# Softplus terms summed by TensorE in the first batch, and two scan carries copied at once, in a two-layer vision network on one core

## The chip, the cores and the metric

The kernel runs on one core of one Trainium2 chip. The metric is the device time of one execution in microseconds, as the median of repeated runs. All matrices are FP32.

## What is computed

The network has two layers; each mixes positions and then channels, with residuals between. Only the first half of layer 0 is touched here. It is a selective scan in four directions (k = 0 to 3) over an image of 32 x 32 positions (L = 1024), with D = 384 channels and N = 16 states, for a batch of 4:

```python
x_dbl = einsum('bkdl,kcd->bkcl', xs, x_proj_weight)      # 12 + 16 + 16 rows
dts   = einsum('bkrl,kdr->bkdl', x_dbl[:, :, :12], dt_projs_weight)
dt    = softplus(dts + dt_projs_bias)
# scan over l, for every channel d and state n:
h = h * exp(dt * A) + (dt * u) * B ;  y = sum_n h * C
```

After the scan come a merge of the four directions, a LayerNorm and a GELU. The rest of the network is a mixture of experts (two of four experts per token), an attention with eight heads, and a factored feed-forward. This document calls that rest of a batch its tail.

## The kernel before

**Units.** The scan layer works through 32 units in order: batch b (4), direction k (4), half of the positions i (2, each HF = 512 wide). The two halves of one direction follow each other. The first starts from a zero state and stores the last state of every block in `carry`; the second starts from `carry`. So units 0, 2, 4 and so on (the first-half units) copy carries, and units 1, 3, 5 do not. Units 0 to 7 are the first batch.

**Inside a unit** (`chunk`). Three chunks of 128 channels; in each, four groups g of four states. In a group, a tile covers 32 channels x 4 states on 128 partitions, and there are four blocks of 512 positions, in two pairs q:

- GpSimd (POOL) makes `bx = dtr * B` for both blocks of a pair in one instruction (L408). `bx` has six buffers, so three groups can be under way.
- ScalarE (ACT) makes `da = exp(dtr * nega)` for one block, into PSUM (L417; two banks).
- VectorE (DVE) runs the scan of one block (L422). For q = 0 the state goes over `bx`, for q = 1 over `da`.
- For q = 0, in a first-half unit, VectorE copies the last column of each of the two blocks from `bx` to `carry` (L433, one element per partition, SBUF to SBUF, one instruction a block); then POOL multiplies both blocks by C in place (L436). For q = 1 VectorE copies the last column from `da` in PSUM (L428) and multiplies by C itself (L429).
- TensorE (PE) sums the states with a selection matrix into the accumulator `acc` (L443), which frees `bx`. At the end of a chunk VectorE adds `acc` into `y` (L282, L286).

**One unit ahead** (`project`). While a unit is scanned, a generator prepares the next one. It is advanced once per group. Its first step makes the 44 rows of `x_dbl` (L318, copied by L322) and sends B and C through DRAM (`bcs`). Then, for each of three chunks of channels, it makes dt and dt * u. `begin` issues a product into the PSUM tile `ps` (L344) and six activations (L347 to L352). With z the biased product, m = exp(-|z|) and e = 1 + m, softplus is relu(z) + ln(e) + (m - (e - 1)); the last bracket gives back what was rounded off e. One group later POOL does the two subtractions (L364, L365). One group after that VectorE adds the result to relu (L370) and multiplies by u (L371), ACT copies dt out (L372), and the SP queue stores both to DRAM (L373, L374), from where the next unit's `dtr` tiles are loaded (L392). So the project part of units 1 to 7 is issued inside units 0 to 6, and that of unit 0 before the loop, with no scan beside it. Unit 7 prepares the first unit of the second batch.

**What sets the order.** The instructions of each engine are put in order when the kernel is built, by a scheduler that goes by the program's order as priority and by times that it estimates; on the chip each engine works through its list in that order. `behind` (`issue_after`) puts the POOL subtractions and the VectorE pair of `project` behind the latest group's own instruction on that engine. The product L344 and the activations have no such rule. After a batch's scan its tail is issued too, in part with raised priority, and runs beside the scan of the batches after it. The tail of the last batch has nothing beside it.

**Room.** The tag `ps` has two PSUM banks, for `acc`, `dt_ps`, `xd_ps` and the LayerNorms. The tag `k2` has six SBUF tiles of 128 x 512, for `wdt`, `xd`, `mag`, `one_e` and `lnw`. `d` and `du` are the tiles of `mag` and `one_e`, used again. All eight PSUM banks are taken.

Of the kernel before, what the change touches and what calls it, by code (L numbers as in the profile page):

```python
# [11 lines left out]
AF = mybir.ActivationFunctionType  # L12
# [98 lines left out]
def halves(i):  # L111
    return slice(i * HF, (i + 1) * HF)


class Body:
# [76 lines left out]
    def scan_layer(self, x1, between):  # L192

        nc, tc, a = self.nc, self.tc, self.a
        with ExitStack() as ctx:
# [58 lines left out]
            for n, unit in enumerate(units):  # L254
# [3 lines left out]
                if n + 1 < len(units):  # L258
                    nb = units[n + 1][0]
                    if nb not in us:  # L260
                        us[nb] = start(nb)
                    project = self.project(units[n + 1], us[nb], wx, work, dram, psum, ahead)
                    next(project)
# [29 lines left out]
    def project(self, unit, u, wx, work, dram, psum, made):  # L293

        nc, a = self.nc, self.a
        b, k, i = unit
        by_cols = k % 2 == 1  # L300
        w = slice(i * (HW // NH), (i + 1) * (HW // NH))

        def part(c):
            if by_cols:
                return u[:, c, :].rearrange("p (h w) -> p w h", h=HW)[:, w, :]
            return u[:, c, halves(i)]

        def split(ap):
            return ap.rearrange("p (w h) -> p w h", h=HW) if by_cols else ap

        def k2(name, shape=(P, HF)):
            return work.tile([*shape], F32, tag="k2", name=name, bufs=6)

        wdt = k2("wdt", (R, D))
        nc.sync.dma_start(out=wdt, in_=a["wdt"][:, k, :])
        ps = psum.tile([P, HF], F32, tag="ps", name="xd_ps")
        for c in range(DC):
            nc.tensor.matmul(  # L318
                split(ps[:XD, :]), wx[:, c, k, :], part(c), start=(c == 0), stop=(c == DC - 1)
            )  # L320
        xd = k2("xd", (XD, HF))
        nc.scalar.copy(xd, ps[:XD, :])  # L322
        rows = dram.tile([2 * NS, HF], F32, tag="rows", name="rows")
        nc.sync.dma_start(out=rows, in_=xd[R:XD, :])
        view = rows.rearrange("(t g n) l -> n t g l", t=2, g=NG)
        bcs = []
        for g in range(NG):
            bc = work.tile([P, 2, HF], F32, tag="bcs", name="bcs", bufs=5)
            for n in range(NJ):
                nc.sync.dma_start(  # L330
                    out=bc[n * DB : (n + 1) * DB], in_=view[n, :, g].partition_broadcast(DB)
                )
            bcs.append(bc)

        dd = dram.tile([2, D, HF], F32, tag="dd", name="dd")
        made += [bcs, dd]
        yield  # L340

        def begin(c):
            ps = psum.tile([P, HF], F32, tag="ps", name="dt_ps")
            nc.tensor.matmul(ps, wdt[:, c * P : (c + 1) * P], xd[:R, :], start=True, stop=True)  # L344
            bias = self.col("dtb", k * DC + c)
            mag, one_e, lnw = k2("mag"), k2("one_e"), k2("lnw")
            nc.scalar.activation(mag, ps, AF.Abs, bias=bias)  # L347
            nc.scalar.activation(ps, ps, AF.Relu, bias=bias)
            nc.scalar.activation(mag, mag, AF.Exp, scale=-1.0)
            nc.scalar.activation(one_e, mag, AF.Identity, bias=1.0)  # L350
            nc.scalar.activation(lnw, one_e, AF.Ln)
            nc.scalar.activation(one_e, one_e, AF.Identity, bias=self.minus1)  # L352
            return ps, mag, one_e, lnw

        def behind(engine):
            if self.place_behind is None:
                return nullcontext()
            return self.tc.issue_after(self.place_behind[engine])

        for c in range(DC):  # L360
            ps, mag, one_e, lnw = begin(c)
            yield
            with behind("pool"):
                nc.gpsimd.tensor_sub(mag, one_e, mag)  # L364
                nc.gpsimd.tensor_sub(lnw, lnw, mag)  # L365
            yield
            d, du = mag, one_e
            rows = slice(c * P, (c + 1) * P)
            with behind("dve"):
                nc.vector.tensor_add(ps, ps, lnw)  # L370
                nc.vector.tensor_mul(split(du), split(ps), part(c))  # L371
            nc.scalar.copy(d, ps)  # L372
            nc.sync.dma_start(out=dd[0, rows, :], in_=d)  # L373
            ins = nc.sync.dma_start(out=dd[1, rows, :], in_=du).ins  # L374
        made.append(ins)

    def chunk(self, unit, first, c, fed, carry, nega, sel, acc, work, dap):

        nc = self.nc
        b, k, i = unit
        bcs, dd, _ = fed
        dtr = []
        for q in range(NJ // 2):

            pair = []
            at = c * P + q * 2 * DB
            for s in range(2):
                t = work.tile([P, 2, HF], F32, tag="dtr", name="dtr", bufs=7)  # L390
                for n in range(NJ):
                    nc.sync.dma_start(  # L392
                        out=t[n * DB : (n + 1) * DB],
                        in_=dd[s, at : at + 2 * DB, :].rearrange("(j d) l -> d j l", d=DB),
                    )
                pair.append(t)
            dtr.append(pair)

        def run(ap):
            return ap[:, ::-1] if k >= 2 else ap  # L400

        last = 0 if k >= 2 else HF - 1
        for g in range(NG):
            bc = bcs[g]
            out = []
            for q in range(NJ // 2):
                bx = work.tile([P, 2, HF], F32, tag="bx", name="bx", bufs=6)
                pool = nc.gpsimd.tensor_mul(  # L408
                    bx, dtr[q][1], bc[:, 0].unsqueeze(1).to_broadcast([P, 2, HF])
                ).ins  # L410
                cg = bc[:, 1]
                at = ((c * 2 + q) * NG + g) * 2
                for j in range(2):
                    block = c * NJ + 2 * q + j
                    col = (k * NB + block) * NG + g
                    da = dap.tile([P, HF], F32, tag="da", name="da")
                    nc.scalar.activation(  # L417
                        da, dtr[q][0][:, j, :], AF.Exp, scale=nega[:, col : col + 1]
                    )
                    hold = carry[:, at + j : at + j + 1]  # L420
                    h = bx[:, j, :] if q == 0 else da
                    nc.vector.tensor_tensor_scan(  # L422
                        run(h), run(da), run(bx[:, j, :]), 0.0 if first else hold,
                        ALU.mult, ALU.add,
                    )
                    if q == 1:
                        if first:
                            nc.vector.tensor_copy(hold, h[:, last : last + 1])  # L428
                        dve = nc.vector.tensor_mul(bx[:, j, :], h, cg).ins  # L429
                if q == 0:  # L430
                    if first:
                        for j in range(2):
                            nc.vector.tensor_copy(  # L433
                                carry[:, at + j : at + j + 1], bx[:, j, last : last + 1]
                            )
                    pool = nc.gpsimd.tensor_mul(  # L436
                        bx, bx, cg.unsqueeze(1).to_broadcast([P, 2, HF])
                    ).ins
                out.append(bx)
            for q in range(NJ // 2):  # L440
                for j in range(2):
                    lo = (2 * q + j) * DB
                    nc.tensor.matmul(  # L443
                        acc[lo : lo + DB, :], sel, out[q][:, j, :],
                        start=(g == 0), stop=(g == NG - 1),
                    )
            self.place_behind = {"pool": pool, "dve": dve}
            yield
# [485 lines left out]
    def attention(self, xc, sums, room):  # L934
# [71 lines left out]

        steps = [(t, i, j) for t in range(HEADS // 2) for i in range(NH) for j in range(MB)]
        made = [project(0)]
        ahead = scores(0, made[0][0], 0, 0)
        atts = []  # L1010
# [363 lines left out]
```

## Time and profile before

| | us |
|---|---|
| median of three runs (4611.89 to 4616.29) | 4612.92 |
| the profiled execution | 4613.12 |
| its span, first to last instruction | 4611.1 |
| busy in the span: PE / DVE / ACT / POOL | 3353.1 / 3031.5 / 2543.8 / 3096.2 |
| mean granted TensorE clock, of 1 | 0.811 |
| L364 and L365, 96 each, all four batches | 122.0 and 122.4 |
| L370, 96 | 66.0 |
| L433 and L428, 384 each | 52.0 and 56.7 |

How to read it: a line such as "L433 DVE COPY carry<-bx ... x384" is a group: source line, engine, operation, the tile written and those read, the shapes, and the count. Busy time is the time in which an engine carried out an instruction; idle time is put down to what ended it. The slices divide the span into 40 parts of 115 us, with the busy share in tenths. A timeline line has the start in us, the duration in us, the engine, the source line and the operation; "x3" means three instructions in a row. The first batch's scan lies between about 66 and 700 us, the scan of the other three between about 760 and 3650 us, and after that comes the last tail.

### The profile page before, as it was taken

To read this page: it belongs to the slowest core of one execution; us is meant where nothing else is said; L and a number is where in the kernel's file an instruction comes from. 1 tells how busy PE (TensorE), PEld (TensorE's weight loads), DVE (VectorE), ACT (ScalarE), POOL (GpSimd) and SP (SyncE) were. 2 spreads that over 40 slices of the span, in tenths; PEclk is the share of its full clock that TensorE was granted. 3 is DMA by queue.
4 is the path that set the end of the run, shared out by engine and by line. 5 is a ranking of instruction groups with operands and counts; after the bars stand their busy time and mean duration, and the time that the engine had idled before them with its cause. 6 is when DMAs were issued, how large, how long until landed. Compare 5 with 4: busy or idle time off the path is not lost.

```text
span 4611.1 us, 46660 instructions
## 1 busy us (share of the span) xinstructions
PE 3353.1 (73%) x13660; PEld 1599.6 (35%) x13660; DVE 3031.5 (66%) x4368; ACT 2543.8 (55%) x4406; POOL 3096.2 (67%) x1515
## 2 busy tenths in 40 slices
PE   4333334549995788659998587846999679999696
PEld 1000001225553232325554222314555335556333
DVE  4888887777887876978887678895878720001101
ACT  4545454536665667466666476556666543434454
POOL 5999997778998877778998578867989610000100
PEclk6565555569997888769998788857999789999897
DMA  3343353557877533456879434444789553334200
GB/s 112 112 126 105 98 148 95 148 168 207 236 232 212 147 96 103 134 160 192 228 218 282 124 97 114 114 126 155 218 233 264 157 173 99 125 115 167 72 16 15
DMA packets 404359, 684.78 MB, mean 149 GB/s; under 512 B 50944, under 2 KB 206464, under 8 KB 404096
## 3 DMA queue, kind: packets, MB, share of 16 engines
q1 hardware_dynamic: 395360, 656.16, 48.9%
q0 software_dynamic: 8192, 25.17, 1.7%
q8 instruction: 109, 1.79, 0.2%
q14 instruction: 154, 1.26, 0.1%
q10 hardware_dynamic: 544, 0.40, 0.0%
HBM read 561.47 MB, written 120.06 MB: 148 GB/s over the span
## 4 chain that ended last, share of the span: by engine, by line
PE 35%; DVE 23%; POOL 11%; ACT 10%; DMA 9%; issue 9%; SPq 2%; another core or an unknown queue 1%; DVEq 0%; POOLq 0%; ACTq 0%
PE y_ps L883 8%; DVE bx L422 7%; DVE da L422 7%; PE h_ps L867 7%; POOL bx L408 6%; PE s_ps L975 4%; DMA dtr<-dd 4%; PE o_acc L1024 3%; POOL bx L436 3%; PE acc L443 3%; ACT da L417 3%; DVE bx L429 3%; PE o_ps L1071 2%; DMA bcs<-rows 1%; PE xd_ps L318 1%
## 5 line engine op out<-in xcount | busy, mean ns | idle before, releaser
L408 POOL TENSOR_TENSOR bx<-dtr,bcs 128x1024 f32<-128x1024 f32 x768 | 1795.8, 2365 | 207.7 <-PE acc L443 153.8
L417 ACT ACTIVATE da<-dtr,nega 128x512 f32<-128x512 f32 x1536 | 1048.6, 693 | 1104.8 <-DVE bx L429 635.2
L436 POOL TENSOR_TENSOR bx<-bx,bcs 128x1024 f32<-128x1024 f32 x384 | 902.8, 2358 | 227.9 <-DVE bx L422 100.1
L443 PE MATMUL acc<-bx,sel 128*32 128x512 f32 x3072 | 551.5, 757 | 537.5 <-POOL bx L436 413.5
L867 PE MATMUL h_ps<-xc,w 128*128 128x256 f32 (+1 forms) x3168 | 675.5, 368 | 50.7 <-DVE xc L849 26.5
L883 PE MATMUL y_ps<-w,hs 128*128 128x384 f32 x1824 | 649.7, 509 | 67.3 <-ACT hs L876 61.9
L867 PEld LDWEIGHTS h_ps<-xc,w 128*128 128x128 f32 x3168 | 553.8, 199 | 244.3 <-issue 107.1
L422 DVE TENSOR_TENSOR_SCAN bx<-da,carry,bx 128x512 f32<-128x512 f32 x384 | 473.6, 1268 | 158.9 <-POOL bx L408 96.4
L422 DVE TENSOR_TENSOR_SCAN bx<-da,bx 128x512 f32<-128x512 f32 x384 | 452.2, 1209 | 124.2 <-POOL bx L408 80.8
L429 DVE TENSOR_TENSOR bx<-da,bcs 128x512 f32<-128x512 f32 x768 | 510.3, 679 | 4.3
L422 DVE TENSOR_TENSOR_SCAN da<-da,carry,bx 128x512 f32<-128x512 f32 x384 | 477.1, 1271 | 54.3 <-ACT da L417 38.5
L422 DVE TENSOR_TENSOR_SCAN da<-da,bx 128x512 f32<-128x512 f32 x384 | 453.8, 1217 | 69.6 <-ACT da L417 41.8
L883 PEld LDWEIGHTS y_ps<-w,hs 128*128 128x128 f32 x1824 | 352.6, 198 | 355.9 <-issue 75.2
L980 ACT ACTIVATE ex<-s_ps 128x512 f32<-128x512 f32 x512 | 300.4, 592 | 281.2 <-PE s_ps L975 261.5
L443 PEld LDWEIGHTS acc<-bx,sel 128*32 128x32 f32 x3072 | 82.9, 120 | 875.7 <-POOL bx L436 564.7
L975 PE MATMUL s_ps<-w 64*128 64x512 f32 x1024 | 308.4, 679 | 84.7 <-ACT ex L980 84.6
L1065 POOL TENSOR_TENSOR xt<-xt,wb 128x3072 f32<-128x3072 f32 x4 | 26.8, 6694 | 421.7 <-DMA wb<-in_wb 421.7
L1024 PE MATMUL o_acc<-ex,vt 128*64 128x512 f32 x1024 | 296.8, 660 | 0.0
L872 ACT ACTIVATE hs<-h_ps,bb 128x256 f32<-128x256 f32 (+1 forms) x528 | 194.1, 449 | 99.1 <-PE h_ps L867 98.7
L901 POOL DMA_INDIRECT got<-made,g_pos x64 | 60.8, 950 | 227.6 <-PE h_ps L1111 207.1
L344 PE MATMUL dt_ps<-xd,wdt 12*128 12x512 f32 x192 | 137.0, 800 | 83.9 <-ACT mag L372 46.0
L887 DVE TENSOR_TENSOR y<-y_ps,bb 128x384 f32<-128x384 f32 x76 | 41.6, 547 | 231.0 <-PE y_ps L883 230.8
(206 smaller groups left out, 3858.1 us busy)
## 6 DMA issues: line engine op xcount, KB each, us to landing
w<-in_w SPq DMA_DIRECT2D x352, 576.0 KB
dtr<-dd SPq DMA_DIRECT2D x1536, 128.0 KB
bcs<-rows SPq DMA_DIRECT2D x512, 128.0 KB
dd<-one_e SPq DMA_DIRECT2D x96, 256.0 KB
dd<-mag SPq DMA_DIRECT2D x96, 256.0 KB
rows<-zero SPq DMA_DIRECT2D x76, 192.0 KB
xs<-rows SPq DMA_DIRECT2D x32, 384.0 KB
made<-y SPq DMA_DIRECT2D x32, 384.0 KB
```

The source lines that it names most:

```text
L408: pool = nc.gpsimd.tensor_mul(bx, dtr[q][1], bc[:, 0].unsqueeze(1).to_broadcast([P, 2, HF])).ins
L417: nc.scalar.activation(da, dtr[q][0][:, j, :], AF.Exp, scale=nega[:, col : col + 1])
L422: nc.vector.tensor_tensor_scan(run(h), run(da), run(bx[:, j, :]), 0.0 if first else hold, ALU.mult, ALU.add,)
L429: dve = nc.vector.tensor_mul(bx[:, j, :], h, cg).ins
L436: pool = nc.gpsimd.tensor_mul(bx, bx, cg.unsqueeze(1).to_broadcast([P, 2, HF])).ins
L443: nc.tensor.matmul(acc[lo : lo + DB, :], sel, out[q][:, j, :], start=(g == 0), stop=(g == NG - 1),)
L867: nc.tensor.matmul(ps[:, r, :], w1[(f + r) // wf][:, c, (f + r) % wf * P : ((f + r) % wf + 1) * P], xc[:, c, :], start=(c == 0), stop=(c = ...
L872: nc.scalar.activation(hs[:, f + r, :], ps[:, r, :], AF.Identity, bias=bb[:, f + r : f + r + 1])
L883: nc.tensor.matmul(out[:, :D], hs[:, f, t * P : (t + 1) * P], w2[f // wf][:, f % wf, :], start=(f == 0), stop=(f == FC - 1),)
L975: nc.tensor.matmul(ps[:, o, :], w[rows, j * P : (j + 1) * P], w[rows, halves(i)], start=True, stop=True,)
L980: ins = nc.scalar.activation(ex[:, o, :], ps[:, o, :], AF.Exp, scale=HD**-0.5, accum_out=sums[:, t, 2 * j + o, i : i + 1],).ins
L1024: ins = nc.tensor.matmul(out[cols, :], made[t][1][:, j, cols], ex[:, o, :], start=(j == 0), stop=(j == MB - 1),).ins
```

## The change

For the first batch (b = 0) relu goes to an SBUF tile of its own, the last activation gives 1 - e, and TensorE adds the four terms into the bank that held z, as four products with the identity: ln(e), 1 - e, m, relu. POOL's two subtractions and VectorE's add are left out there. For the other batches nothing changes in this part. In `chunk`, for all batches, the two one-element carry copies of q = 0 become one instruction, which copies the last column of both blocks.

```diff
+            relu = k2("relu") if b == 0 else ps
             nc.scalar.activation(mag, ps, AF.Abs, bias=bias)
-            nc.scalar.activation(ps, ps, AF.Relu, bias=bias)
+            nc.scalar.activation(relu, ps, AF.Relu, bias=bias)
             nc.scalar.activation(mag, mag, AF.Exp, scale=-1.0)
             nc.scalar.activation(one_e, mag, AF.Identity, bias=1.0)
             nc.scalar.activation(lnw, one_e, AF.Ln)
-            nc.scalar.activation(one_e, one_e, AF.Identity, bias=self.minus1)
+            if b == 0:
+                nc.scalar.activation(one_e, one_e, AF.Identity, bias=1.0, scale=-1.0)
+                terms = [lnw, one_e, mag, relu]
+                for t in terms:
+                    nc.tensor.matmul(
+                        ps, self.ident, t, start=(t is terms[0]), stop=(t is terms[-1])
+                    )
+            else:
+                nc.scalar.activation(one_e, one_e, AF.Identity, bias=self.minus1)
...
-            with behind("pool"):
-                nc.gpsimd.tensor_sub(mag, one_e, mag)
-                nc.gpsimd.tensor_sub(lnw, lnw, mag)
+            if b > 0:
+                with behind("pool"):
+                    nc.gpsimd.tensor_sub(mag, one_e, mag)
+                    nc.gpsimd.tensor_sub(lnw, lnw, mag)
...
             with behind("dve"):
-                nc.vector.tensor_add(ps, ps, lnw)
+                if b > 0:
+                    nc.vector.tensor_add(ps, ps, lnw)
                 nc.vector.tensor_mul(split(du), split(ps), part(c))
...
-                        for j in range(2):
-                            nc.vector.tensor_copy(
-                                carry[:, at + j : at + j + 1], bx[:, j, last : last + 1]
-                            )
+                        nc.vector.tensor_copy(carry[:, at : at + 2], bx[:, :, last])
```

## The prediction

> **What bounds the kernel now.** I read the page's slices first, then the table by stretches, the groups and waits of the first batch, single lines of VectorE, and last the chain of waits. The page says that no one engine bounds the whole span: PE is busy 73%, POOL 67%, DVE 66%, ACT 55%. The slices and the table show stages.
>
> ```profile
> DVE  4888887777887876978887678895878720001101
> POOL 5999997778998877778998578867989610000100
> PEclk6565555569997888769998788857999789999897
> ```
> ```profile
> 66.00:700.00 634.00, 231.51 (x739) 35.62 (x737) 552.94 (x754) 313.52 (x488) 631.14 (x295) 0.56 0.43 118
> 700.00:1035.00 335.00, 164.44 (x597) 80.95 (x598) 251.19 (x381) 150.44 (x230) 253.76 (x129) 0.60 0.48 138
> 1035.00:3650.00 2615.00, 2098.85 (x8728) 1036.87 (x8726) 2072.77 (x2870) 1632.98 (x2790) 2134.67 (x1019) 0.86 0.61 176
> ```
>
> The table's columns are PE, PE's weight loads, DVE, ACT, POOL (each with its count), the granted clock, DMA share and GB/s. From 66 to 700 us, the first batch's scan, POOL is busy 631 of 634 us and is the bound; DVE has 13% idle, PE 63%. From 1035 to 3650 us PE, DVE and POOL each have about 80%, and none bounds alone. In the chain of waits of that stretch the scan lines of VectorE have 9.1 + 9.0 + 3.5 = 21.6% (L422 twice, L429), 565 us of the 1671 us for which they are busy there: 34% of VectorE's scan work ends on the chain.
>
> The other thing to see is what VectorE does while POOL runs.
>
> ```profile
> L433 DVE COPY carry<-bx x384: 94/148/155, 68.3 to 3550.4; 128x1 f32<-128x1 f32 x192
> L637 DVE TENSOR_SCALAR xt<-xt,mv,rstd x32: 466/473/2554, 910.3 to 3749.3; 128x384 f32<-128x384 f32 x32
> L703 DVE TENSOR_TENSOR g_run<-g_run,g_cnt x32: 136/161/2341, 945.5 to 3755.0; 128x4 f32<-128x4 f32 x32
> L792 DVE CAST g_expert<-g_ef x4: 141/164/2295, 960.6 to 3757.8; 128x11 int32<-128x11 f32 x4
> L766 DVE CAST g_pos<-g_picked x4: 174/175/1531, 967.3 to 3759.3; 128x16 int32<-128x16 f32 x4
> ```
> ```profile
> 910.34 7.17 POOL L408 TENSOR_TENSOR bx<-dtr,bcs 128x1024 f32<-128x1024 f32 x3
> 910.35 9.11 DVE L637 TENSOR_SCALAR xt<-xt,mv,rstd 128x384 f32<-128x384 f32 x5
> 917.48 1.37 POOL L365 TENSOR_TENSOR lnw<-lnw,mag 128x512 f32<-128x512 f32 x1
> ```
>
> The three numbers are min/median/max ns. A scalar operation of 0.47 us takes up to 2.55 us, casts of 11 and 16 elements 0.15 or 2.3 us. In the timeline each stretched one ends within 0.3 us of the end of a POOL instruction: of the 32 instructions of L637, 10 start while POOL runs, and all 10 are stretched. Between 910 and 917 us VectorE gets in once after each POOL instruction. The one-element copies of L433 are never stretched: none of 384 is over 155 ns, with POOL busy nearly throughout.
>
> **The change, part by part** (base: the profiled execution, 4613.1 us with a span of 4611.1; the median of the runs is 4612.9, so the two may be used alike).
>
> *POOL's two subtractions, first batch.* 24 chunks lose L364 and L365. One costs 1.23 us from start to next start (660.41 to 661.64 us in POOL's timeline). Three chunks belong to the start-up; 21 are issued in the scan units 0 to 6, three per unit. POOL's unit: 12 groups of three big products at 2.32 us (six of L408 in 13.87 us, two of L436 in 4.64) are 83.5 us, six subtractions 7.4 us: 90.9 us, as observed (168 of L408, 24 a unit, in 634 us: 90.6). So POOL could give back 7 x 7.4 = 52 us. Unit 7 prepares the second batch and keeps its subtractions.
>
> *VectorE's add L370.* 24 of 0.69 us go, and with them its waits for POOL (17.5 us between 100 and 690 us). No gain of their own while POOL is the bound; they give VectorE room.
>
> *TensorE's sums.* 24 x 4 FP32 products with the identity, each of two instructions. Nearest rows: six instructions of L318 take 5.35 us when PE had idled 13 us (430.92 us) and 2.77 us when it came straight from other matmuls (327.82 us). Eight take 3.7 to 7.1 us: 21 x 3.7 to 7.1 = 78 to 149 us more PE work in 634 us, of which 402 are free. Nothing of it is on the path unless it blocks: the first two products wait for ACT's last terms (one_e ends about 8 us after the dt product), and the acc matmuls L443 stand behind them in PE's queue; they free the bx buffers for POOL's L408. Six buffers hold three groups, some 21 us of POOL, and POOL waits for acc 2.6 us in that stage now. I take 0.5 us a chunk, 10 us; ends 0 and the full 7.1 us x 21 = 149. VectorE's product L371 stays where it was issued, two groups later, so the terms have about 14 us; without that cover it would wait up to 7.1 us.
>
> The Trainium skill ("TensorE: Matmul & The Clock Gate", Part 1) says that the array runs at half clock until it has been busy for about 3.4 us; by that an eight-instruction burst would cost an estimated 5.1 us, between my two rows, and the sum would stay.
>
> *ACT.* Relu writes SBUF, not PSUM: by Abs, which does so already, 0.68 against 0.66 us, 24 x 0.02. The last term with a constant bias: 0.63 (L350) against 0.72 us. Both sides under 3 us in all and behind other waits: 0. The fourth k2 tile fills the ring of six (wdt, xd and four), so the next chunk's one_e or lnw may wait for the dd stores; the store now releases lnw for 8.4 us in all. 0 to 3 us a chunk; 0 taken, as Abs of the next chunk starts 2.9 us after the copy that feeds the last store (304.54 to 307.42 us).
>
> *Start-up.* Before the scan starts, nothing hides the first chunk. After its last ACT term: two subtractions and the add, 48.9 to 52.4 us = 3.5 us, against three products, 2.8 to 5.4 us: -1 to +2; I take +2.
>
> *The merged copy.* 192 groups (48 in the first batch) lose one copy, 0.13 us each: 0.27 us for the pair at 329.88 us. The new instruction copies two elements of SBUF to SBUF; no row shows one. From below it is the one-element copy, 0.15 us, no wait. From above it is stretched as the casts of 11 and 16 elements are. I take the stretched side: like them it is a one-source operation over more than one element, both ends in SBUF. At the 137 pairs of L433 that stand side by side in the trace, POOL is inside an instruction in 119 (0.87), with 1.19 us to go on average. Waits are longer where POOL's next instruction gets in first (L519 once took 8.96 us): over fourteen of VectorE's lines in SBUF, the 32 stretched cases that are not directly behind another add 2.25 us on average. I take 1.7 us, the middle of 1.19 and 2.25. Behind the waiting copy VectorE holds the next two scans, the products L429, and POOL's L436 needs the copy done.
>
> The Trainium skill speaks against this edit: "Vector Engine (DVE) Microarchitecture Reference", 5.1, has a one-source operation in SBUF with two elements per partition run in its two-port mode. "SBUF — State Buffer", Who interferes with whom, has that mode hold the port pair shared with GpSimd, the loser blocked for a whole instruction. By these pages every merged copy can wait; by the row of L433 alone none would, and the sum below would end at the second rival's 4567.
>
> **The sum.** First-half units (0, 2, 4, 6), VectorE: a group takes 6.02 us (317.14 to 323.16 us), 5.89 with one copy fewer; 12 groups 70.7, L371 and the add into y 3 x 1.7 = 5.1, waits for ACT and PE that stay (27 us in 6.5 units) 4: 79.8 us. The waits add 12 x 1.7 x 0.86 = 17.5: 97.3 us, over POOL's 83.5. VectorE becomes the bound: +6.4 x 4 = +26 us. Second-half units (1, 3, 5) copy no carries and follow POOL: -7.4 x 3 = -22 us. Start-up +2. The 10 us of PE waits fall on POOL, which has slack in four units of seven: 3 x 3 x 0.5 = +4 (4.5). First batch: +10 us. Later batches: 144 x (0.87 x 1.7 - 0.13) = 194 us more on VectorE, of which 34% ends on the chain: +66 us. Together +76: 4613 + 76 = **4689 us**. With 1.19 us a wait it is 4644: first batch -22 + 6 + 2 = -14, later 144 x 0.91 x 0.34 = +45. With 2.25 us, and half of it on the chain, it is +25 and +132: 4770.
>
> **Rivals.**
> 1. *The copies wait, but cheaply*: VectorE has slack behind the copy (20% idle after 1035 us). With 10% on the chain, 194 us make +19, and the first batch -14: 4618.
> 2. *No wait at all* (two elements behave as one): the 52 us of POOL come back, less 10 for PE, +2 start-up, -0.13 x 144 x 0.34 = -6: -46, 4567 us; faster, the other side from my forecast. It decides if the copy's wait averages under about 0.6 us. For it: 384 one-element copies without a stretch. Against it: 10 of 10 in L637, and the casts.
> 3. *PE's queue*: no wait at the copy, but the products hold up acc and so POOL's buffers. At 7.1 us for each of 21 chunks: 149 - 52 = +97, 4710; it beats the gain from 2.5 us a chunk. Against it: PE idles 8 to 13 us between acc bursts, and three groups of buffers lie between.
>
> **Chances.** Forecast 0.60, rival 1 0.12, rival 2 0.20, rival 3 0.08. Slower by over 0.2% (9 us, what this measurement can tell from no change): 0.54 + 0.03 + 0 + 0.07 = 0.64; within: 0.04 + 0.05 + 0.03 + 0.01 = 0.13; faster: 0.02 + 0.04 + 0.17 = 0.23. The forecast's own range is 4640 to 4770. The 8-in-10 range reaches down into rival 2, to 4565, and up to 4760.
>
> **What would show it.** The copy's line: min 0.15 us, mean over 1 us, max over 2.3 us; the one-element copies of L428 unchanged. POOL's share from 66 us on falls below 95% in first-half units and stays at 99% in second-half ones; the first batch's scan still ends near 700 us (near 655 in rival 2). POOL's waits for acc stay under 20 us in that stage (over 100 in rival 3). A copy that stays under 0.2 us would refute me; so would copies that wait while the later batches take the time they took.

## The result, and the profile after

| | median us (lowest to highest, runs) |
|---|---|
| before | 4606.31 (4597.30 to 4616.29, 9) |
| after | 4637.68 (4620.47 to 4645.02, 9) |
| ratio after / before | 1.0061, 95% interval 1.0046 to 1.0076 |

The change makes the kernel slower by 0.6%, some 28 us (0.0061 x 4606) or 31 us by the difference of the medians. The forecast was +76 us. In the profiled executions the span goes from 4611.1 to 4633.9 us, +22.8 us; the steps below are compared on that figure.

The page's slices after the change (115.8 us each, busy share in tenths, and the granted TensorE clock):

```profile
DVE  4999998767888876978888787896778830002101
POOL 4999998687988875768988678868787820000100
PEclk7766665579997898769998788867999889999897
```

The table by stretches, with the columns of the one in the prediction:

```profile
66.00:700.00 634.00, 344.37 (x998) 94.59 (x996) 595.96 (x713) 326.21 (x509) 598.31 (x259) 0.68 0.47 124
700.00:1035.00 335.00, 172.77 (x633) 84.56 (x634) 260.38 (x362) 152.09 (x233) 255.86 (x130) 0.64 0.48 142
1035.00:3650.00 2615.00, 2054.90 (x8544) 1015.68 (x8546) 2125.74 (x2680) 1590.82 (x2730) 2080.84 (x993) 0.86 0.60 174
```

From 66 to 700 us POOL is no longer full: 598 of 634 us, for 631 before. VectorE rises from 553 to 596 and is now level with it. PE goes from 232 to 344, and its granted clock from 0.56 to 0.68. From 1035 to 3650 us VectorE has 53 us more of busy time, while PE, ACT and POOL have less: in the same stretch less work gets through.

The lines of VectorE that copy carries in the kernel after, the merged copy (L444) and the one-element copy from PSUM (L440, L428 before); the numbers are min/median/max ns:

```profile
L444 DVE COPY carry<-bx x192: 134/774/9125, 65.1 to 3592.6; 128x2 f32<-128x2 f32 x192
...
L440 DVE COPY carry<-da x384: 99/144/160, 69.0 to 3596.6; 128x1 f32<-128x1 f32 x192
```

And the timeline of the kernel after in the first unit (start us, duration us, engine, line; "x6" is six in a row):

```profile
84.48 13.89 POOL L420 TENSOR_TENSOR bx<-dtr,bcs 128x1024 f32<-128x1024 f32 x6
...
89.24 2.23 DVE L444 COPY carry<-bx 128x2 f32<-128x2 f32 x1
...
98.32 2.34 POOL L445 TENSOR_TENSOR bx<-bx,bcs 128x1024 f32<-128x1024 f32 x1
99.15 1.53 DVE L444 COPY carry<-bx 128x2 f32<-128x2 f32 x1
...
100.83 2.35 POOL L445 TENSOR_TENSOR bx<-bx,bcs 128x1024 f32<-128x1024 f32 x1 [0.17 <-DVE carry L444]
```

The copy that starts at 99.15 ends at 100.68; the GpSimd instruction over it ends at 100.66. The one at 89.24 ends with the third of the six. Over the whole trace GpSimd is inside an instruction when 127 of the 192 copies start. Of these 116 are stretched (taken as over 0.25 us, for 0.16 us undisturbed); the mean over the 127 is 1.60 us, and each stretched one ends 22 to 30 ns after a GpSimd instruction does. Ten of them let more than one instruction of GpSimd go first (the longest 9.1 us). None of the other 65 is stretched. The group's mean is 1.113 us, its sum 213.6 us; the 384 single copies of before were busy for 52.0 us.

**Where the time went.** The scan has 48 instructions on VectorE in each unit, so the start of every 48th marks the units. All in us, from the profiled executions; the rows e1 to e10 are the experiments that follow.

| | unit 0 starts | units 0, 2, 4, 6 | units 1, 3, 5 | unit 7 | unit 8 starts | units 8 to 31 | last tail | span |
|---|---|---|---|---|---|---|---|---|
| before | 66.0 | 367.4 | 270.0 | 116.4 | 819.8 | 2829.6 | 961.6 | 4611.1 |
| after | 62.2 | 374.8 | 244.5 | 96.7 | 778.3 | 2932.6 | 923.0 | 4633.9 |
| e1 | 66.0 | 341.6 | 250.8 | 97.3 | 755.7 | 2854.2 | 923.8 | 4533.7 |
| e2 | 63.1 | 342.3 | 250.5 | 97.3 | 753.1 | 2794.8 | 962.2 | 4510.1 |
| e3 | 65.8 | 389.9 | 267.9 | 116.9 | 840.4 | 2891.2 | 913.8 | 4645.4 |
| e4 | 62.9 | 344.8 | 249.2 | 97.4 | 754.4 | 2933.2 | 922.9 | 4610.5 |
| e9 | 62.2 | 394.7 | 267.9 | 115.1 | 839.9 | 2897.4 | 944.5 | 4681.8 |
| e10 | 64.4 | 379.6 | 245.5 | 96.8 | 786.2 | 2835.7 | 940.9 | 4562.8 |

So the change has two halves of opposite sign. The first batch ends 41.5 us earlier; from unit 8 to the end the kernel takes 3855.6 us for 3791.3, 64.3 us more. The table also corrects the bounds given ahead of the prediction: before the change units 0 to 6 end at 703 us, but unit 7, still of the first batch, runs to 820 us, and only there does the second batch's scan begin.

### The profile page after: what moved, and what is told of

It is laid out like the page before. It is cut to its first block, busy times and chain, and to the rows that moved or that the text cites. A ratio compares the mean times of both kernels' runs of the same rounds, so it can differ in the third digit from the quotient of the medians.

```text
span 4633.9 us, 46751 instructions
## 1 busy us (share of the span) xinstructions
PE 3455.2 (75%) x13852; PEld 1645.3 (36%) x13852; DVE 3170.7 (68%) x4152; ACT 2536.0 (55%) x4406; POOL 3041.0 (66%) x1467
## 5 line engine op out<-in xcount | busy, mean ns | idle before, releaser
L445 POOL TENSOR_TENSOR bx<-bx,bcs 128x1024 f32<-128x1024 f32 x384 | 903.7, 2356 | 308.3 <-DVE carry L444 134.9
L452 PE MATMUL acc<-bx,sel 128*32 128x512 f32 x3072 | 529.0, 714 | 354.0 <-POOL bx L445 251.9
L984 PE MATMUL s_ps<-w 64*128 64x512 f32 x1024 | 318.3, 692 | 103.8 <-ACT ex L989 103.4
L444 DVE COPY carry<-bx 128x2 f32<-128x2 f32 x192 | 213.6, 1113 | 5.0
L345 PE MATMUL dt_ps<-xd,wdt 12*128 12x512 f32 x192 | 126.5, 744 | 78.0 <-ACT mag L384 26.2
```

Source lines behind the costliest of these rows:

```text
L444: nc.vector.tensor_copy(carry[:, at : at + 2], bx[:, :, last])
L445: pool = nc.gpsimd.tensor_mul(bx, bx, cg.unsqueeze(1).to_broadcast([P, 2, HF])).ins
L452: nc.tensor.matmul(acc[lo : lo + DB, :], sel, out[q][:, j, :], start=(g == 0), stop=(g == NG - 1),)
L984: nc.tensor.matmul(ps[:, o, :], w[rows, j * P : (j + 1) * P], w[rows, halves(i)], start=True, stop=True,)
```

## The experiments

Theory L: a copy of two elements from SBUF to SBUF waits for the end of GpSimd's running instruction, a copy of one element does not; these waits cost more than TensorE's sums gain. The rivals: TensorE's products make the kernel slow through PE's queue (the third rival of the prediction; Q in the expectations), or what is dear about the merged copy is the order that the scheduler builds round it, not the wait (P). A second theory, U, came up on the way: unit 7's gain comes from the one buffer `u`, which is free earlier.

The first four ran in one set, e5 to e8 in another, e9 and e10 in a third, each with runs of the kernel before beside them (medians 4602.23, 4606.71 and 4573.09: on the chip of the third set the kernel before is 0.7% faster). Ratios are against those; a quotient of ratios from two sets supposes that both kernels change alike from chip to chip. Unit times and spans are those of single executions, and the runs of one kernel lie up to 28 us apart.

**e1: the merged copy without its wait.** The kernel after, with the copy issued as a reduction over one element, which has the same operands and the same result:

```diff
-                        nc.vector.tensor_copy(carry[:, at : at + 2], bx[:, :, last])
+                        nc.vector.tensor_reduce(
+                            carry[:, at : at + 2], bx[:, :, last : last + 1], AX.X, ALU.max
+                        )
```

> The changed kernel, with its 192 merged carry copies issued as a reduction by maximum over one element (same two elements in, same two out, one instruction). The queues of VectorE, ScalarE, GpSimd and the DMA issues keep the changed kernel's order exactly; TensorE's differs in six rows in the last tail. Reductions were never stretched in the trace of before. Theory L (the two-element copy waits for GpSimd's running instruction): the line falls from a mean of 1.11 us to about 0.17 us with no case over 0.3 us; first-half units of the first batch fall from 94 us to 85 us (4 x -9 = -36 us); the later batches lose their 144 x 0.95 us on VectorE, a third to a half of it on the chain (-45 to -65 us). Total 4637 - 80 to 100 = 4537 to 4557 us. Theory P (the new order of the queues makes the difference, the waits are hidden): within 10 us of the changed kernel, 4627 to 4647 us. Theory Q (products in TensorE's queue hold the buffers): also 4627 to 4647 us.

Measured: 4544.92 us, ratio 0.9867 (0.9845 to 0.9889). The traces show the instructions of the kernel after in the same order, but for a few places on PE and one on VectorE, where a copy and a two-element memset change places; what differs is the form of these 192 instructions. Their line in e1:

```profile
L444 DVE TENSOR_REDUCE carry<-bx x192: 124/155/159, 68.9 to 3491.2; 128x2 f32<-128x2 f32 x192
```

GpSimd is inside an instruction when 150 of the 192 start, and none goes over 159 ns. The Trainium skill ("SBUF — State Buffer", Who interferes with whom) says that a copy can take the port pair that VectorE shares with GpSimd, and that on trn2 a reduction never contends; the two lines, 9125 and 159 ns at most with the same operands, agree. So the wait belongs to the copy's form. Taking it out is worth 1.0061 / 0.9867 = 1.0197, about 91 us (the half widths of both intervals, added as squares, give 1.017 to 1.022). Without it the change would have been a gain of 1.3%. The total is as expected, the parts nearly: units 0, 2, 4 and 6 lose 33 us, for 36 expected, and the rest from unit 8 on 77.7, for 45 to 65.

**e2: TensorE's sums alone** (the two one-element copies put back).

```diff
-                        nc.vector.tensor_copy(carry[:, at : at + 2], bx[:, :, last])
+                        for j in range(2):
+                            nc.vector.tensor_copy(
+                                carry[:, at + j : at + j + 1], bx[:, j, last : last + 1]
+                            )
```

> TensorE's sums in the first batch, the two one-element copies of before kept. Theory L: as the reduction, less 0.13 us for each of 192 copies of which few are on a chain: 4540 to 4565 us, the units 0 to 6 at 81 to 86 us each against 90 to 92 us before, the first batch done 50 us or more earlier. Theory P: the queues are in a third order, so the later batches may go either way by 20 us or so, but no gain is tied to the copies. Theory Q: slower than before, over 4620 us, with GpSimd's waits for acc over 50 us in the first batch.

Measured: 4513.94 us, ratio 0.9811 (0.9792 to 0.983): 26 us under the expectation. It is the fastest of all kernels here, so this half of the change is a clear gain, and the rival of PE's queue falls. The first batch ends like e1's, within 3 us, and has the same order of instructions; the rest takes 3757.0 us against e1's 3778.0, with no waiting copy in either. There the scheduler's order differs between e1 and e2 on every engine, which is the likely cause; no run shows it.

**e3: the merged copy alone**, on the kernel before.

> Before, with the merged copy alone; GpSimd keeps its subtractions. Theory L: the copy's mean is about 1.1 us; first batch: GpSimd still needs 90.9 us a unit and VectorE, with 12 x 0.9 us more, comes to about 92 us, so 0 to +10 us in all; later batches +45 to +100 us. Total 4650 to 4715 us. Theory P: within 20 us of before, 4590 to 4630 us, while the copies wait as long.

Measured: 4648.66 us, ratio 1.0098 (1.0079 to 1.0117), just under the expected range. The copies wait as in the kernel after (mean 1.041 us). The first batch, whose instructions stand in the order of the kernel before on VectorE, ACT, POOL and PE, ends 20.6 us later (0 to 10 were expected), and all of it comes in units 0, 2, 4 and 6 (+22.5), the ones that copy carries.

**e4: the kernel after with single copies in the first batch**, so that 144 merged ones stay, in batches 1 to 3.

```diff
+                        if b > 0:
                             nc.vector.tensor_copy(carry[:, at : at + 2], bx[:, :, last])
+                        else:
+                            for j in range(2):
...
```

> The changed kernel with one-element copies in the first batch and the merged copy in batches 1 to 3. ScalarE's queue is in the changed kernel's order exactly, GpSimd's and VectorE's nearly. Theory L: the first-half units of the first batch fall to 85 us (-36 us), the later batches stay as in the changed kernel: 4595 to 4610 us if the gain is kept to the end. Theory P: as the changed kernel, 4627 to 4647 us.

Measured: 4607.87 us, ratio 1.0015 (1.0002 to 1.0028), as expected. The first batch is e2's (754.4 and 753.1 us), the rest is that of the kernel after (3856.1 and 3855.6). The two halves can be had one without the other. e4 and e1 ran in one set and have the same order after the first batch, but for the places named at e1: the 144 waits from unit 8 on cost 1.0015 / 0.9867 = 1.0150, about 69 us, and eat the whole gain of the sums.

**e5 and e6: where the sums' gain lies.** Unit 7 shrank by 20 us, and the prediction had given it nothing. It prepares batch 1 and keeps its subtractions. But the input tile `u` has one buffer: batch 1's `u` is loaded when the first batch's last product with `u` (L371) is done, and its LayerNorm comes after that. In the kernel before (SP and PE, then POOL):

```profile
704.59 0.41 SPq L221 DMA_DIRECT2D u<-in_x  x1
...
711.93 5.18 PE L157 MATMUL ln_mean<-u,ones 128*128 128x512 f32 x6 [5.35 <-DMA u<-in_x]
```
```profile
696.41 1.25 POOL L365 TENSOR_TENSOR lnw<-lnw,mag 128x512 f32<-128x512 f32 x1
...
749.68 13.89 POOL L408 TENSOR_TENSOR bx<-dtr,bcs 128x1024 f32<-128x1024 f32 x6 [19.56 <-PE acc L443]
```

The last subtraction ends at 697.7 us behind POOL's big products; add and product follow, and the load is issued at 704.6, after unit 7 has begun (703.4). The LayerNorm then stands between the accumulators of unit 7, and POOL idles 19.6 us for `acc`. To separate this from POOL's own saving, e5 makes TensorE's sums only in the project part of unit 7 (issued in unit 6), e6 in all the others:

```diff
+        summed = b == 0 and k == KG - 1 and i == 0            # e5
+        summed = b == 0 and (k < KG - 1 or i > 0)             # e6
...
-            relu = k2("relu") if b == 0 else ps
+            relu = k2("relu") if summed else ps
```

Both have single copies; the name `summed` stands at the other places of the change too. In both, units 0 to 6 stand for POOL's saving and unit 7 for U.

> Before, with TensorE's sums only in the project part of unit 7 (3 of 24 chunks, issued inside unit 6); all copies single. Theory U (unit 7 loses its 19 us because the last product that reads u no longer queues behind GpSimd, so that the one u buffer is reloaded some 30 us ahead of unit 7): units 0 to 5 as before (90 to 93 us), unit 6 about 84 us, unit 7 about 97 us in place of 116 us, unit 8 starts 25 us earlier than before, and u is asked for near 675 us, not at 704.5 us. Total about 4577 us if that is kept, by 35 us either way for the new order of the later batches. Rival R (unit 7's 19 us come from GpSimd's relief over all seven units, or from a luckier order): unit 7 stays at 110 us or more.

> The complement: sums in the project parts of units 0 to 6, GpSimd's subtractions and VectorE's add in that of unit 7. Theory U: units 0 to 5 at 83 to 90 us as with all sums, unit 6 near 90 us, unit 7 at 115 us as before, u asked for at the end of unit 6; unit 8 starts 40 to 47 us earlier than before, not 67. Total about 4560 us, by 35 us either way. Rival R: unit 7 near 97 us all the same, unit 8 65 us earlier.

Measured: e5 4557.9 us, ratio 0.9892 (0.9877 to 0.9908); e6 4524.83 us, ratio 0.9829 (0.9814 to 0.9843), at the low end of what was expected.

| | units 0 to 6 | `u` load issued | unit 7 | unit 8 starts |
|---|---|---|---|---|
| before | 637.4 | 704.6 | 116.4 | 819.8 |
| e5 | 640.3 | 675.6 | 96.6 | 803.2 |
| e6 | 597.4 | 662.2 | 113.3 | 774.0 |

In e5, with one unit's sums, unit 7 falls by 19.8 us and nothing else does. Its POOL in unit 7 waits for `acc` like this:

```profile
727.96 6.98 POOL L421 TENSOR_TENSOR bx<-dtr,bcs 128x1024 f32<-128x1024 f32 x3 [0.54 <-PE acc L456]
...
763.61 4.67 POOL L421 TENSOR_TENSOR bx<-dtr,bcs 128x1024 f32<-128x1024 f32 x2 [4.14 <-PE acc L456]
```

The wait of 19.6 us is gone. In e6 it is still there, and unit 7 stays at 113.3:

```profile
703.85 13.89 POOL L421 TENSOR_TENSOR bx<-dtr,bcs 128x1024 f32<-128x1024 f32 x6 [21.51 <-PE acc L456]
```

The other kernels agree: in the seven where the load goes out 26 to 31 us ahead of unit 7, that unit takes 96.6 to 97.4 us; in the five where it goes out 1 to 2 us behind its start, 113.3 to 116.9. So POOL's subtractions in unit 6 delay the load, and unit 7 pays for it. That the one buffer holds the load back is read off the program and the trace (in the kernel before the last L371 ends at 703.5 us, the load is issued 1.1 us later), not tested by itself: a second buffer for `u` wasn't tried. That e5's unit 6 would take 84 us was a miss (93.1), and its unit 8 started 17 us earlier, not 25.

**e7: the reduction on the kernel before** (as e1, without the sums).

> Before, with the merged carry copy as a reduction (one instruction, two elements) and no sums by TensorE. It takes the wait away and keeps the merging. Theory L alone: nothing is left to cost anything, 192 x 0.13 us less on VectorE, first batch as before within 5 us, total 4590 to 4605 us. Theory P2 (one instruction fewer also moves the order of the later batches, as the 31 us between the reduction with sums and the single copies with sums suggest): first batch as before, the later batches 20 to 40 us longer, total 4620 to 4640 us.

Measured: 4611.34 us, ratio 1.0017 (1.0006 to 1.0027): between the two expectations. The first batch is that of before (unit 8 starts at 819.6 for 819.8), so the merged instruction without a wait gains nothing there; the rest takes as long too (3791.2 for 3791.3), though its parts differ (scan 33.5 longer, tail 33.6 shorter). Against e3 the waits cost 1.0098 / 1.0017 = 1.0081, only 37 us. But e3 and e7 differ in 10 to 28% of the places of their orders too, by engine, all of them behind 2765 us of e3. Up to unit 23 the order is the same, and e3 comes there 49.0 us later (2654.0 for 2605.0), with 136 us added to 144 copies: 36%. From there to the end 14 us of it are lost again.

**e8: U used twice more.** e2, with the sums also in the last unit of batches 1 and 2 (`summed = b == 0 or (k == KG - 1 and i == 0)`).

> TensorE's sums in the first batch, single copies, and the sums also in the project part of the last unit of batches 1 and 2 (6 more chunks), to release u earlier there. Theory U: u for the batches 2 and 3 is asked for 10 to 30 us ahead of the units 15 and 23 and these get 5 to 20 us shorter each; total 4480 to 4510 us against 4514 us with the sums in the first batch alone. Against it: TensorE is 80% busy there with the tail, and six bursts of 3.7 to 7 us add 22 to 42 us to it: 4514 to 4540 us.

Measured: 4550.27 us, ratio 0.9883 (0.9867 to 0.9899), worse than e2, and outside what either side expected. The scan ended at 3506.1 us for e2's 3547.9, 42 us earlier; the last tail then took 1038.6 us for 962.2. What the scan gained, the tail gave back and more, presumably because less of the last tail's work ran beside the scan. Which part of it was put off was not followed further. Of U's own signs one came and one did not. `u` for batch 2 goes out 24.7 us ahead of unit 15, where e2 asks for it 0.4 us behind that unit's start, and unit 15 takes 114.3 us for 119.9. For batch 3 it goes out 9.7 us ahead of unit 23 (e2: 5.8), and unit 23 takes 151.4 us for 134.0. So beside the tails of earlier batches an earlier load did not always shorten the unit.

**e9 and e10: the same waits in one order.** e3 and e7 left open what the waits cost over the whole run, since orders differed. These two keep the orders of before (e9) and of e2 (e10), instruction by instruction (the traces show one pair exchanged on PE), and only widen the second copy of each pair to two adjacent columns, of which one is used:

```diff
-                        for j in range(2):
-                            nc.vector.tensor_copy(
-                                carry[:, at + j : at + j + 1], bx[:, j, last : last + 1]
-                            )
+                        nc.vector.tensor_copy(carry[:, at, own : own + 1], bx[:, 0, last : last + 1])
+                        nc.vector.tensor_copy(carry[:, at + 1, :], bx[:, 1, two])
```

> This kernel is the one before, with one thing widened: of each pair of single copies, the second copies two adjacent elements of its block (one of them used), so that 192 copies of two elements stand in the kernel before's own order of instructions, and 192 of one element beside them. Theory L (a copy of two elements on VectorE waits for the end of GpSimd's instruction, and what that costs depends on the slack of the order it stands in): the two-element copies have a mean of about 1.1 us, the one-element copies stay near 0.14 us; the first batch, bound by GpSimd, ends 0 to 20 us later; the median is 4625 to 4685 us against some 4605 for the kernel before. Rival (what made the merged copies dear was the new order that the planner chose round them, or a source that lies in two blocks): the two-element copies stay under 0.3 us, or wait as much and the median stays within 10 us of the kernel before.

> This kernel is the one with TensorE's sums and single copies (e2), with the second copy of each pair widened to two adjacent elements, one of them used. Theory L: the two-element copies have a mean of about 1.0 us; units 1 to 5, which now have GpSimd and VectorE nearly level, take 84 to 95 us for 83; the first batch ends 15 to 30 us later, and the whole 50 to 95 us later than e2's 4514: 4565 to 4610 us. Rival: the waits are bought by slack here, and the median stays within 15 us of e2; or the price is the same as in the kernel before (under 20 us apart).

Measured: e9 4677.79 us, ratio 1.0223 (1.0209 to 1.0236), some 103 us and above the expected 20 to 80; e10 4566.02 us, ratio 0.9975 (0.9962 to 0.9987), 77 us over e2 by the ratios and within the expected 50 to 95, though its first batch ends 33 us later than e2's, for 15 to 30 expected. In e9 the two forms stand side by side, the two-element line first:

```profile
L434 DVE COPY carry<-bx x192: 129/632/7696, 64.6 to 3635.4; 128x2 f32<-128x2 f32 x192
...
L433 DVE COPY carry<-bx x192: 95/127/156, 64.5 to 3635.3; 128x1 f32<-128x1 f32 x192
```

and in its timeline, VectorE and then POOL:

```profile
110.64 0.13 DVE L433 COPY carry<-bx 128x1 f32<-128x1 f32 x1
110.76 2.25 DVE L434 COPY carry<-bx 128x2 f32<-128x2 f32 x1
112.93 2.33 DVE L423 TENSOR_TENSOR_SCAN da<-da,bx 128x512 f32<-128x512 f32 x2
```
```profile
110.64 2.34 POOL L435 TENSOR_TENSOR bx<-bx,bcs 128x1024 f32<-128x1024 f32 x1
```

Under one GpSimd instruction, from 110.64 to 112.98, the one-element copy runs in 0.13 us and the two-element one ends with it, at 113.01; the scan waits behind it. So the width of the copy is the cause, and a source in two blocks is not needed.

With these runs the same 192 waits have four prices, and the 144 of the later batches one more. The time added to the copies is their number x (mean with a wait less mean without); the price is the quotient of the ratios, times 4605 us. By the intervals of the ratios each price is good to 6 to 12 us. e9 and before, and e4 and e1, ran in one set; the other rows join two:

| pair | order | added to the copies | ratio | price | share |
|---|---|---|---|---|---|
| e9 / before | the same | 192 x 0.905 = 174 us | 1.0223 | 103 us | 59% |
| after / e1 | the same but for the places named at e1 | 192 x 0.960 = 184 | 1.0197 | 91 | 49% |
| e10 / e2 | the same | 192 x 1.002 = 192 | 1.0167 | 77 | 40% |
| e3 / e7 | the same up to unit 23, then each its own | 192 x 0.887 = 170 | 1.0081 | 37 | 22% |
| e4 / e1, later batches alone | as after / e1 | 144 x 0.944 = 136 | 1.0150 | 69 | 51% |

In a fixed order 36 to 59% of the waiting ends in the span. Where the scheduler built another order the price came out lower once; a difference of that size is also what orders alone can make: the kernels whose copies do not wait (before, e1, e2, e5 to e8) take 3744 to 3791 us from unit 8 to the end, 47 us apart, with the same or nearly the same work there. (These are single executions, so part of the 47 us is their spread.)

## Why the prediction was wrong

The sign was right and so was the mechanism; the size was off, +76 us for +22.8 in the profiled spans. Two steps of the sum failed: unit 7 was given no gain, and the first batch's waits were priced too high. Term by term, with the unit table:

| term | predicted | measured, after less before |
|---|---|---|
| units 0, 2, 4, 6, with PE's waits | +26 and +4 | +7.4 |
| units 1, 3, 5 | -22 | -25.5 |
| unit 7 | 0 | -19.7 |
| start-up | +2 | -3.8 |
| first batch | +10 | -41.5 |
| later batches | +66 | +64.3 |

*POOL's subtractions* were right. Units 1, 3 and 5 gave back 8.5 us each for 7.4, and in e1 and e2, without waits, units 1 to 5 fall to 82.7 to 84.6 us, at POOL's 83.5.

*Unit 7* is the step that failed by omission. "Unit 7 prepares the second batch and keeps its subtractions" is true, but its bound was not POOL's work: the unit held a wait of 19.6 us for `acc`. That wait stands in the trace of before (the line shown with e5 and e6), but the sum had no term for the stretch from 700 to 1035 us in which it lies. The subtractions in unit 6 held `u` up; e5 and e6 show it.

*The merged copy's wait* was mis-sized. Predicted: 0.87 x 1.7 = 1.48 us on each copy. Measured: 0.66 (127 of 192) x 1.44 (1.60 less the 0.16 of an undisturbed copy) = 0.95. One share, that of the pairs which stand side by side, was taken for all stages. In the trace of before GpSimd runs at the start of all 48 pairs of the first batch, but of 105 of the 144 later ones (73%); among the 46 later pairs that stand apart, and were left out, it is 25. The wait also thins itself out: POOL's product L445 needs the copy, so POOL idles behind it, and later copies can find it idle. In e1, with nearly the same order and no wait, 150 of the 192 start under a GpSimd instruction, in the kernel after 127. POOL's waits in the kernel after between 66 and 660 us:

```profile
POOL bx L445 <- DVE carry L444: 17.5, 22, 2.8
POOL bx L420 <- PE acc L452: 7.6, 4, 4.0
```

In the first batch the copies' mean is 1.035 us, 0.885 over a single copy. With that the prediction's own sum for a first-half unit is 79.8 + 12 x 0.885 = 90.4 us, not 97.3; measured are 93.7 (374.8 / 4), 1.9 over the 91.9 of before instead of 6.4. VectorE did come to the front there, as forecast. Unit 2 in the kernel after, and then in e1, where the copies do not wait (columns as in the table by stretches):

```profile
242.50:336.20 93.70, 47.27 (x138) 12.49 (x140) 89.56 (x115) 45.27 (x71) 86.84 (x38) 0.66 0.44 110
```
```profile
238.60:321.90 83.30, 43.57 (x132) 10.87 (x132) 77.65 (x115) 45.24 (x71) 83.30 (x37) 0.66 0.48 122
```

VectorE is busy 89.6 of 93.7 us and POOL 86.8, where without the wait POOL is busy throughout. POOL's share is 87, 93, 92 and 97% in units 0, 2, 4 and 6, and 96, 99 and 100% in units 1, 3 and 5, for "below 95%" and "99%" in the prediction.

*The later batches* came out right by two errors. The waits added 144 x (1.139 - 0.153) = 142 us, not 194. Of these some 69 us (e4 against e1, by the ratios) to 78 us (3855.6 less e1's 3778.0, in the profiled spans) ended in the span, 49 to 55% and not 34%. What is left of the +64.3, up to 13 us the other way (3778.0 for 3791.3), is within the spread of runs: e1's six lie 28 us apart. So the agreement of +66 with +64.3 is luck. The share of VectorE's scan lines on the chain of waits gave too low a price for a wait put on VectorE in the middle of a group; the next two scans, POOL's product and then PE all stand behind it, which is the likely reason. The prediction's upper end has a slip too: with 2.25 us a wait its own terms give about +33 us for the first batch, not +25.

*TensorE's sums* were right. The eight instructions take 6.4 us a chunk (47.3 + 42.7 + 35.9 + 27.6 us for 24 chunks), within 3.7 to 7.1 and above the estimate of 5.1; POOL's waits for `acc` are 7.6 us, under the 20 named. VectorE's product waits 5.6 us for them between 100 and 690 us, where its add waited 17.5 us for POOL before: that wait was traded for a smaller one.

*Start-up*: -3.8 us says little, as e9, whose start-up is that of before, also began at 62.2 us.

*The rivals.* The second, no wait at all, was named with its place: "if the copy's wait averages under about 0.6 us". The copy's mean is 1.1 us, and e1, which takes the wait away, is what that rival describes: unit 7 starts at 658.4 us there, for 655 named, and the whole is 1.3% faster, for 1.0% named. The first rival, that the copies wait cheaply, named 4618; the outcome lies between it and the forecast, but not for its reason: the waits are not cheap, some 69 to 78 us in the later batches, and the first batch's gain of 41.5 us paid for more than half of them.

## What to carry to other kernels

An instruction saved on VectorE can cost more than it saves if the merged form has to wait for GpSimd: here a reduction over one element, or two one-element copies, did the same work without a wait. Price a new wait from the stage where most of its instances are, and from what stands behind it, not from an engine's average share of the chain of waits. And look at the boundary between stages for a single buffer whose last reader is delayed by the engine that is being relieved: its earlier release goes with 19 of the 64 us that the sums gained in the first batch (before against e1).

## What the hardware showed that was not expected

- The granted clock of TensorE rose with its work: 0.56 from 66 to 700 us before, 0.68 after, 0.67 in e1 and e2, 0.58 in e5, where only one unit makes the sums.
- A waiting copy can lose to several GpSimd instructions in a row: 9.1 us at most in the kernel after, 13.3 us in e10, with instructions of about 2.35 us:

```profile
L446 DVE COPY carry<-bx x192: 149/688/13275, 67.3 to 3516.4; 128x2 f32<-128x2 f32 x192
```

- One element against two decides it: 0 of 384 one-element copies of before over 155 ns, 118 of the 126 two-element copies of e9 that met a running GpSimd instruction stretched.
